# Layer 3's attention: where weights and first rows lie, when queries are masked, and the rhythm of the experts' steps

## The chip, the cores and the metric

The kernel runs on one core of one Trainium2 chip. A core has five engines with queues of their own: PE (TensorE, matrix products), DVE (VectorE), ACT (ScalarE), POOL (GpSimd) and SP (SyncE, which here only issues transfers). They share an on-chip memory (SBUF, 128 partitions) and the accumulators of PE (PSUM, eight banks). The metric is the device time of one execution in microseconds (us); a lower time is better. The version before takes 1958.88 us, the median of 4 runs.

## The reference

Four layers follow each other on 16 sequences (NB) of 256 tokens (T) with 128 features (D). Each layer normalises its input and adds to it an attention and a feed-forward part:

```python
xn = layernorm(x)
x = x + attention(xn) + ffn(xn)
```

The change is in layer 3. Its attention has 16 heads of 8 features. Queries with little energy are set to zero before the scores, and softmax is taken over all 256 keys:

```python
q, k, v = split(xn @ w_qkv.T + b_qkv)               # 16 heads of hd = 8
energy = norm(q, axis=-1)
mask = energy > energy.mean() * 0.1
scores = einsum('bihd,bjhd->bijh', q, k) / sqrt(hd) * mask[:, :, None, :]
probs = softmax(scores, axis=2)                     # over the keys j
attention = einsum('bijh,bjhd->bihd', probs, v) @ w_out.T + b_out
```

Its feed-forward part sends every token to the one of 8 experts (128 to 512 to 128 features, ReLU between) whose gate is largest.

## The kernel before

Tokens are kept as 32 blocks of 128 (X, partition = token in its block). Layer 3 has three stages.

**The front** (L2431 to L2584) normalises X to XN (norm, L2440, even blocks on DVE, odd ones on ACT), transposes four blocks at a time to xnT (turn, L2451), multiplies them by the weights (products, L2456: qT and kT feature-major, V token-major, and the gate logits L), and takes the energies EN (energy, L2480). Eight such groups g of 512 tokens follow each other. Then comes the routing: the threshold thr, the mask of the first queries, counts per expert with products pcnt and pcum, and from them pos, the slot of every token, and ewi, the rows of the experts' weights. A mask(g) (L2415) is one DVE operation that zeroes the queries of one group in qT, and one store of them to DRAM (q_d) on SP. heads_in(g) (L2421) loads queries and keys of the group (two sequences) back from q_d and k_d into QEs and KEs, with 8 features and a row of maxima on each quarter of the partitions. The front ends with 32 scatters on POOL (L2579), which write the rows of XN to their slots (xs_d), one after the other.

**The loop** (L2761 on, U, LAG and LATE are set there) runs u from -6 to 67. Steps 0 to 63 are the four steps s of each sequence b. A step has two halves (par), each with two heads' transposed scores pE (PE), their exponentials PT (ACT), and, six steps ahead (LAG), the same heads' scores pM, of which DVE takes the row maxima mx (L2781). values (L2614) multiplies the exponentials of the step before by V into pc, copies pc to cs every second step and sends it through DRAM (c_d) to Y and den; divide, spread and project finish a sequence. The steps u = -6 to -1 compute pM and mx alone: they are called the lead here. maxima_out (L2639) sends the maxima to the queries' spare row.

**The experts** are a generator. For each of NTL = 23 tiles of 256 slots POOL gathers the tile's weights ex and loads its rows xt, PE multiplies in 5 steps (pt, two ph, pf, po), and POOL scatters the result yo to ya_d. The loop takes one step (next(moe)) in each half once the count of halves exceeds LATE; u = 0 has the halves 13 and 14. After the 115th step rows_in (L2728) loads the results in four parts, waits two further steps and adds a part to X in each of four steps.

What sets the order. Within layer 3 the instructions of DVE, PE and ACT run in the order in which the program emits them (manual_schedule); the order on SP and POOL is chosen by a scheduler. Tiles lie in pools that are laid out one behind the other. The first use of a new pool waits for the last use of every older pool whose room it overlaps, in SBUF as in PSUM. Before the change, l3_big (qT, XN, V, EN, pos, ewi, thr) lies over the room of layer 2's large tiles (l2_big), and l3_w (weights, VEs, QEs, KEs, slot) partly over that of layer 2's temporaries (l2_tmp: statistics, accumulated rows, hidden tiles). The front's PSUM pool l3_ps has two banks each with tags t (transposes, pt) and q (pq, pcnt, pbo), two banks for v and one for e (energies, pcum). The loop's pool l3_ps2 takes all eight banks again, so the first pM waits for the last reader of the front's, the bias add of L2574.

The masks' places, and the steps of the experts, are these lines of the loop:

```python
if 2 <= u + LAG < 8:
    mask(u + LAG)
half += 1
if half > LATE:
    next(moe, None)
```

Of the kernel before, what the change touches and what calls it, by code (L numbers as in the profile page):

```python
# [9 lines left out]
F32 = mybir.dt.float32  # L10
I32 = mybir.dt.int32
AF = mybir.ActivationFunctionType
ALU = mybir.AluOpType
AX = mybir.AxisListType
PSUM = bass.MemoryType.PSUM
DRAM = bass.MemoryType.DRAM

P = 128
NB = 16
T = 256  # L20
D = 128
NT = NB * T // P
# [143 lines left out]
def layer0(tc, I, kit, X):  # L166
# [3 lines left out]
    with ExitStack() as ctx:  # L170
# [51 lines left out]
        stats = {}  # L222
        V, S = nc.vector, nc.scalar

# [6 lines left out]
        def rows_of(th, g):  # L231
            return Xv[:, 4 * g : 4 * g + 4, th, :]

        def norm_stats(th, g, part):
# [6 lines left out]
            for i in (2 * part, 2 * part + 1):  # L241
                V.bn_stats(st[:, i, :], rows_of(th, g)[:, i, :])
                V.bn_aggr(mv[:, i, :], st[:, i, :])
            if part == 1:

                rs = tmp.tile([P, 2, 4], F32, name="rs", bufs=8)
                V.tensor_scalar(rs[:, 1, :], mv[:, :, 1], 1.0 + 1e-6, 1e-11, ALU.mult, ALU.add)
                V.tensor_scalar(rs[:, 0, :], mv[:, :, 1], 1e-5, None, ALU.add)
                rsf = rs.rearrange("q a n -> q (a n)")
# [3 lines left out]
        def norm_rows(th, g):  # L253
# [6 lines left out]
            if th == 0:  # L260
                for i in range(4):
                    V.tensor_scalar(
                        xr[:, i, :], src[:, i, :], mv[:, i, 0:1], rs[:, 1, i : i + 1], ALU.subtract, ALU.mult
# [2102 lines left out]
def layer3(tc, I, kit, X, xs_d, ov):  # L2366
    nc = tc.nc
    H, HD, E, HF = 16, 8, 8, 4
    TS, NTL = L3_TS, L3_NTL
    scale = 1.0 / math.sqrt(HD)  # L2370
    vec, act = nc.vector, nc.scalar
    with ExitStack() as ctx:
        big = ctx.enter_context(tc.tile_pool(name="l3_big", bufs=1))
        wp = ctx.enter_context(tc.tile_pool(name="l3_w", bufs=1))
        tmp = ctx.enter_context(tc.tile_pool(name="l3_tmp", bufs=2))

        qT = big.tile([P, NT * P], F32, name="qT")

        XN = big.tile([P, NT, D + 1], F32, name="XN")
        V = big.tile([P, NT, D], F32, name="V")  # L2380
        EN = big.tile([P, NT * P], F32, name="EN")
        pos = big.tile([P, NT], I32, name="pos")
        ewi = big.tile([P, NTL], I32, name="ewi")
# [14 lines left out]
        boc = wp.tile([P, 1], F32, name="boc")  # L2398
        nc.sync.dma_start(boc, I["L3_attn_b_out"].unsqueeze(1))

        VEs = [wp.tile([P, 2, H, 32], F32, name=f"ve{i}") for i in range(2)]


        QEs = [wp.tile([P, 4, 2 * T], F32, name=f"qe{i}") for i in range(2)]
        KEs = [wp.tile([P, 4, 2 * T], F32, name=f"ke{i}") for i in range(2)]

        slot = wp.tile([P, 2 * NTL], F32, name="slot")
        dram = ctx.enter_context(tc.tile_pool(name="l3_dram", bufs=1, space=DRAM))
        q_d = dram.tile([P, NT * P], F32, name="q_d")
        k_d = dram.tile([P, NT * P], F32, name="k_d")  # L2410
# [4 lines left out]
        def mask(g):  # L2415

            cols = slice(512 * g, 512 * g + 512)
            vec.scalar_tensor_tensor(qT[:, cols], EN[:, cols], thr, qT[:, cols], ALU.is_gt, ALU.mult)
            nc.sync.dma_start(q_d[:, cols], qT[:, cols])
# [13 lines left out]
        with ExitStack() as c1:  # L2433
            en = c1.enter_context(tc.tile_pool(name="l3_en", bufs=1))
            ps = c1.enter_context(tc.tile_pool(name="l3_ps", bufs=2, space=PSUM))
            es = en.tile([P, 8], F32, name="es")
            L = en.tile([P, NT, E], F32, name="L")
            xnT, sq = {}, {}
# [10 lines left out]
                        )  # L2449

            def turn(g):  # L2451
                pn = kit.transpose4(ps, XN[:, 4 * g : 4 * g + 4, 0:D], "t")
                xnT[g] = en.tile([P, 4 * P], F32, name="xnT", bufs=3)
                vec.tensor_copy(xnT[g], pn)

# [23 lines left out]

            def energy(g):  # L2480
                cols = slice(512 * g, 512 * g + 512)
                pe = ps.tile([P, 512], F32, name="pe", tag="e", bufs=1)
                nc.tensor.matmul(pe, kit["group8"], sq[g], start=True, stop=True)
                act.activation(EN[:, cols], pe, AF.Sqrt, scale=float(HD), accum_out=es[:, g : g + 1])

            nc.gpsimd.tensor_scalar(XN[:, :, D], kit["token"], 1.0, None, ALU.add)
            norm(0)
            norm(1)
            turn(0)
            for g in range(8):  # L2490
                if g < 6:
# [23 lines left out]
            et = en.tile([P, 1], F32, name="et")  # L2515
            vec.tensor_tensor(L, L, mx.unsqueeze(2).to_broadcast([P, NT, E]), ALU.is_equal)
            vec.tensor_reduce(et, es, AX.X, ALU.add)
            pt = ps.tile([P, 1], F32, name="pt", tag="t")
            nc.tensor.matmul(pt, kit.ones, et, start=True, stop=True)
            vec.scalar_tensor_tensor(  # L2520
                L, L, -float(E), kit["iota"][:, 0:E].unsqueeze(1).to_broadcast([P, NT, E]), ALU.mult, ALU.add
# [6 lines left out]
            vec.tensor_tensor(OH, L, mx.unsqueeze(2).to_broadcast([P, NT, E]), ALU.is_equal)  # L2528

            OHf = OH.rearrange("p n e -> p (n e)")  # L2530
            pcnt = ps.tile([P, NT, E], F32, name="pcnt", tag="q")
            nc.tensor.matmul(pcnt.rearrange("p n e -> p (n e)"), kit.ones, OHf, start=True, stop=True)
            pcum = ps.tile([P, NT, E], F32, name="pcum", tag="e", bufs=1)
            nc.tensor.matmul(pcum.rearrange("p n e -> p (n e)"), kit["triu"], OHf, start=True, stop=True)
            pbo = ps.tile([P, 1], F32, name="pbo", tag="q")
            nc.tensor.matmul(pbo, wo, bqkv[:, 2:3], start=True, stop=True)
            seg = en.tile([P, E, NT], F32, name="seg")
            nc.gpsimd.memset(seg, 1.0)
# [6 lines left out]
            ni = en.tile([P, E], I32, name="ni")  # L2545
            vec.tensor_scalar(ni, inc[:, :, NT - 1], float(TS - 1), None, ALU.add)
            vec.tensor_scalar(ni, ni, 8, None, ALU.logical_shift_right)
            nt = en.tile([P, E], F32, name="nt")
            vec.tensor_copy(nt, ni)
            end = en.tile([P, E], F32, name="end")  # L2550
# [19 lines left out]
            vec.tensor_reduce(ej, past, AX.X, ALU.add)  # L2570
            vec.tensor_scalar(ej, ej, float(E - 1), float(P), ALU.min, ALU.mult)
            vec.tensor_scalar(ewi, ej, kit["token"][:, 0:1], None, ALU.add)

            vec.tensor_tensor(boc, boc, pbo, ALU.add)  # L2574
            mask(1)
            heads_in(1)
            sent = []
# [8 lines left out]
        with ExitStack() as c2:  # L2586
            exp = c2.enter_context(tc.tile_pool(name="l3_ex", bufs=4))
            at = c2.enter_context(tc.tile_pool(name="l3_at", bufs=2))
            ps = c2.enter_context(tc.tile_pool(name="l3_ps2", bufs=1, space=PSUM))
# [61 lines left out]
            def divide(b):  # L2651
                nc.vector.reciprocal(St.den[b], St.den[b])
# [102 lines left out]
            def work():  # L2755
                yield from experts()
                yield from rows_in()

            moe = work()

            U, LAG, LATE = 4 * NB, 6, 20  # L2761
            half = 0
            for u in range(-LAG, U + 4):
                b, s = divmod(u, 4)
                bm, sm = divmod(u + LAG, 4)
                alone = u < 0 or bm >= NB
                for pars in ((0, 1),) if alone else ((0,), (1,)):

                    Ms, Es = [], []
                    for par in pars:  # L2770
                        tags = "me" if par == pars[0] else "em"
                        if bm < NB:
                            Ms.append((ps.tile([P, 2, 2, T], F32, name="pM", tag=tags[0]), bm, sm, par))
                        if 0 <= u < U:
                            Es.append((ps.tile([P, 2, 2, T], F32, name="pE", tag=tags[1]), b, s, par))
                    scores(Ms, Es)
                    for pM, _, _, par in Ms:
                        if sm == 0 and par == 0:
                            St.mx[bm] = at.tile([P, H, 2], F32, name="mx")
                        h0 = 4 * sm + 2 * par  # L2780
                        vec.tensor_reduce(St.mx[bm][:, h0 : h0 + 2, :], pM, AX.X, ALU.max)  # L2781
                    for pE, _, _, par in Es:
                        if par == 0:
                            St.PT[b, s] = at.tile([P, 4, 2, T], F32, name="PT")
                        r0 = 2 * (1 - par)
                        act.activation(St.PT[b, s][:, r0 : r0 + 2], pE, AF.Exp, scale=scale)  # L2786
                    for par in pars:
                        if par == 0:
                            if 1 <= u <= U:
                                values(*divmod(u - 1, 4))  # L2790
                            if s == 2 and 0 <= b + 1 < NB:
                                act.copy(
                                    VEs[(b + 1) % 2][:, :, :, 0:HD],
                                    V[:, 2 * b + 2 : 2 * b + 4, :].rearrange("p i (h d) -> p i h d", h=H),
                                )
                                maxima_out(b + 1)
                            if s == 0 and b % 2 == 0 and 0 < b // 2 < NB // 2 - 1:
                                heads_in(b // 2 + 1)
                            if 2 <= u + LAG < 8:
                                mask(u + LAG)  # L2800
                        half += 1
                        if half > LATE:
                            next(moe, None)

                        if 0 < b <= NB:
                            if (s, par) == (2, 1):
                                divide(b - 1)
                            if (s, par) == (3, 0):
                                spread(b - 1)
                            if (s, par) == (3, 1):  # L2810
                                project(b - 1)
# [88 lines left out]
```

## Time and profile before

| what | value |
|---|---|
| runs | 1959.68, 1958.08, 1943.73, 1961.63 us; median 1958.88 |
| the profiled execution | own time 1960.44 us, span 1958.5 us, mean granted TensorE clock 0.839 |
| hand-over from layer 2 | last DVE operation of layer 2 at 1459.93, first product pq at 1462.72 us |
| routing on DVE | 1499.3 to 1509.9 us |
| 32 scatters on POOL | 1508.3 to 1548.9 us |
| lead, from its first to the loop's first maxima | 1511.86 to 1571.42 us |
| loop with the experts' steps | to 1928.15 us (last yo) |
| end of the span | 1958.5 us |

The profile is one execution seen by the hardware profiler. A line of its timeline has the start in us, the length, the engine, the source line, the operation, the tile written and the tiles read, the shape, how many instructions are taken together, and in brackets how long the engine was idle before and what ended that. A group's line has the busy time of all its instructions, the mean of one in ns, and the idle time before them with its releasers. "issue" means that nothing in the profile explains the wait, "remote" that the releaser is not known. The span leaves out some 2 us of the execution's own time. A matmul's row gives its dispatch and a modelled end; when it is really done shows only in when those who wait for it go on.

### The profile page before, as it was taken

The numbers are of one execution on the slowest core, as the hardware profiler recorded it, in microseconds if no ns is written. First come the engines' busy times: TensorE is split into PE (matmuls) and PEld (weight loads), VectorE is DVE, ScalarE is ACT, GpSimd is POOL, SyncE is SP. The second block draws the span as 40 slices with busy tenths as digits, with TensorE's granted clock in tenths as the row PEclk, the third lists the DMA queues.
The fourth block names the chain that finished last, engine by engine and source line by source line (L and its number), as shares of the span: only waits on it lengthen the run. The fifth ranks groups of instructions, "written<-read, shape, count | busy, mean of one in ns | idle before, by whom it ended". The sixth has DMA issues, their size and how long they took to land.

```text
span 1958.5 us, 26353 instructions
## 1 busy us (share of the span) xinstructions
PE 1515.1 (77%) x8176; PEld 926.0 (47%) x8176; DVE 1338.5 (68%) x4656; ACT 821.6 (42%) x1908; POOL 635.3 (32%) x901
## 2 busy tenths in 40 slices
PE   6686666676675598999988888687887289999995
PEld 3365455554554453444435454344444145555553
DVE  5688999889888537887855567654366266666663
ACT  3555454555555113223324445343443044454442
POOL 4222312213120323343413030556672613333310
PEclk9667766767676668999998999898988589999998
DMA  3121001000000451101102000022222313333314
GB/s 106 26 83 24 12 14 47 18 11 15 13 16 3 89 106 46 44 22 44 22 0 39 8 1 1 18 43 47 41 57 84 106 58 90 103 100 93 106 54 120
DMA packets 114978, 94.43 MB, mean 48 GB/s; under 512 B 35463, under 2 KB 97799, under 8 KB 114599
## 3 DMA queue, kind: packets, MB, share of 16 engines
q1 hardware_dynamic: 94172, 64.20, 12.8%
q0 software_dynamic: 13056, 26.21, 5.4%
q10 hardware_dynamic: 7610, 2.35, 0.5%
q8 instruction: 65, 1.06, 0.2%
q14 instruction: 75, 0.61, 0.1%
HBM read 55.65 MB, written 37.01 MB: 47 GB/s over the span
## 4 chain that ended last, share of the span: by engine, by line
PE 44%; DVE 11%; POOL 5%; issue 4%; DMA 2%; ACT 1%; another core or an unknown queue 0%; ACTq 0%; SPq 0%; POOLq 0%; DVEq 0%
PE pM L2606 6%; PE pc L2619 3%; PE pf L1433 3%; PE ph L2282 3%; PE pf L2265 2%; PE ph L1425 2%; DVE mx L2781 2%; PE pf L2708 2%; PE pk L1392 2%; PE ph L2701 2%; PE tr L151 2%; POOL tok L2168 1%; PE pk L1391 1%; DVE x L143 1%; PE pE L2606 1%
## 5 line engine op out<-in xcount | busy, mean ns | idle before, releaser
L2781 DVE TENSOR_REDUCE mx<-pM 128x4 f32<-128x1024 f32 x128 | 155.1, 1215 | 129.6 <-PE pE L2606 82.2
L2606 PE MATMUL pM<-ke,qe 31*128 31x256 f32 x1024 | 156.4, 433 | 73.4 <-issue 34.3
L2786 ACT ACTIVATE PT<-pE 128x1024 f32<-128x1024 f32 x128 | 130.3, 1023 | 168.0 <-PE pE L2606 166.2
L2606 PEld LDWEIGHTS pM<-ke,qe 31*128 31x128 f32 x1024 | 95.9, 199 | 115.5 <-DVE mx L2781 55.0
L2606 PE MATMUL pE<-qe,ke 32*128 32x256 f32 x1024 | 147.1, 406 | 0.6 <-issue 0.2
L940 ACT ACTIVATE SA<-e,y 16x1 f32<-16x1 f32 x256 | 74.9, 292 | 132.4 <-DVE e L939 105.3
L976 ACT ACTIVATE iR<-SA,A,CR 16x1 f32<-16x1 f32 x240 | 92.5, 386 | 53.0 <-DVE A L945 37.9
L808 PE MATMUL pP<-KB,M 128*128 128x64 f32 x224 | 61.0, 408 | 49.8 <-ACT M L690 49.8
L1131 POOL TENSOR_SCALAR KA<-KT,aS 128x128 f32<-128x128 f32 x128 | 74.5, 601 | 64.0 <-ACT aS L1103 64.0
L2606 PEld LDWEIGHTS pE<-qe,ke 32*128 32x128 f32 x1024 | 92.2, 187 | 4.5 <-ACT PT L2786 1.8
L740 POOL COPY KB<-K 64x256 f32<-64x256 f32 x30 | 11.8, 395 | 247.5 <-PE pP L808 246.6
L1373 POOL TENSOR_TENSOR kv<-qk,v 128x1024 f32<-128x1024 f32 x32 | 65.8, 2057 | 40.9 <-PE pf L1433 10.9
L808 PEld LDWEIGHTS pP<-KB,M 128*128 128x128 f32 x224 | 50.7, 304 | 59.1 <-ACT M L690 59.0
L1427 ACT ACTIVATE e<-ph,eb 128x512 f32<-128x512 f32 x64 | 44.1, 689 | 76.8 <-PE ph L1425 76.1
L2720 POOL DMA_INDIRECT ya_d<-yo,own x46 | 45.6, 992 | 81.1 <-DVE yo L2718 74.1
L1399 DVE TENSOR_REDUCE y<-pr 128x64 f32<-128x512 f32 x64 | 69.2, 1081 | 2.2
L2619 PE MATMUL pc<-PT,ve 128*32 128x256 f32 x1024 | 70.3, 393 | 0.0
L1392 PE MATMUL pk<-kv,tab 128*128 128x512 f32 x128 | 68.4, 626 | 0.0
L292 PE MATMUL pn<-tab,xn 128*128 128x128 f32 x32 | 14.2, 457 | 69.4 <-POOL xn L284 69.4
L1425 PE MATMUL ph<-xnT,ew 128*128 128x512 f32 x128 | 66.8, 603 | 0.0
L1433 PE MATMUL pf<-e,ew 128*128 128x512 f32 x128 | 64.1, 593 | 0.0
L945 DVE SCALAR_TENSOR_TENSOR A<-CR,e,A 16x33 f32<-16x33 f32 (+3 forms) x240 | 57.5, 240 | 8.5
(603 smaller groups left out, 4210.1 us busy)
## 6 DMA issues: line engine op xcount, KB each, us to landing
WB<-w_d SPq DMA_DIRECT2D x8, 1024.0 KB
c_d<-cs SPq DMA_DIRECT2D x16, 512.0 KB
ew<-in_L_ffn_W SPq DMA_DIRECT2D x16, 256.0 KB
xs_d<-zero SPq DMA_DIRECT2D x1, 2967.0 KB
xt<-xs_d POOLq DMA_DIRECT2D x23, 129.0 KB
xrow_d<-XN SPq DMA_DIRECT2D x4, 548.0 KB
X<-in_x SPq DMA_DIRECT2D x4, 512.0 KB
VA<-v_d SPq DMA_DIRECT2D x64, 32.0 KB
```

The source lines that it names most:

```text
L808: nc.tensor.matmul(Run.pP[p // 4][:, o : o + 64], M[:, p, :], KB[:, p].rearrange("q h k -> q (h k)"), start=p % 4 == 0, stop=False, skip_g ...
L940: nc.scalar.activation(s, e, AF.Sqrt, bias=y, scale=-1.0)
L976: nc.scalar.activation(iR, s, AF.Sqrt, bias=A[:, 17:18], scale=SB[:, t, 17:18])
L1131: nc.gpsimd.tensor_scalar(KA[:, p, :], KT[:, p, :], Run.aS[:, p : p + 1], None, ALU.mult)
L1392: nc.tensor.matmul(pkf, kit["triu"], St.kv[n][:, hs], start=i == 0, stop=True)
L1399: nc.vector.tensor_reduce(St.y[n][:, hh], pr.rearrange("p h e f -> p h f e"), AX.X, ALU.add)
L1425: nc.tensor.matmul(ph, ew1[:, e, k * P : (k + 1) * P], xg, start=True, stop=True)
L1433: nc.tensor.matmul(pf, ew2[:, e, k, :], he[q], start=False, stop=False)
L2606: nc.tensor.matmul(out[:, k, i, :], A[rows, s, c + i * P : c + i * P + P], B[rows, s, c : c + T], start=True, stop=True,)
L2619: nc.tensor.matmul(St.pc[32 * r : 32 * r + 32, s % 2, :], VEs[b % 2][:, k, 4 * s + r, :], St.PT[b, s][:, r, k, :], start=k == 0, stop=k == 1,)
L2781: vec.tensor_reduce(St.mx[bm][:, h0 : h0 + 2, :], pM, AX.X, ALU.max)
L2786: act.activation(St.PT[b, s][:, r0 : r0 + 2], pE, AF.Exp, scale=scale)
```

## The change

Four edits, all in layer3.

1. Rooms. A new pool l3_first with qT and V lies first, then l3_w with the weights alone, then l3_big with the rest, to which VEs, QEs, KEs and slot now belong. The first two lie over l2_big only, and l3_big lies over both l2_big and l2_tmp.
2. Banks. The transposes and pt, pbo get a pool of their own (psT, two banks, 6 and 7), and the energies, pcum and pcnt another (psE, two banks, 4 and 5); q and v lie in banks 0 to 3. The add of the bias boc is moved from behind ewi to before the tiles are counted.
3. Masks. Masks 0 and 1 stay in the front. Masks 2 to 7 move from u = -4 to 1 to u = 4, 12, 20, 28, 36 and 44, each four steps before its heads_in.
4. Experts. LATE is 23 instead of 20, and each 16th half takes a second step.

```diff
+        first = ctx.enter_context(tc.tile_pool(name="l3_first", bufs=1))
+        wp = ctx.enter_context(tc.tile_pool(name="l3_w", bufs=1))
         big = ctx.enter_context(tc.tile_pool(name="l3_big", bufs=1))
-        wp = ctx.enter_context(tc.tile_pool(name="l3_w", bufs=1))
         tmp = ctx.enter_context(tc.tile_pool(name="l3_tmp", bufs=2))
-        qT = big.tile([P, NT * P], F32, name="qT")
+        qT = first.tile([P, NT * P], F32, name="qT")
+        V = first.tile([P, NT, D], F32, name="V")
         XN = big.tile([P, NT, D + 1], F32, name="XN")
-        V = big.tile([P, NT, D], F32, name="V")
...
-        VEs = [wp.tile([P, 2, H, 32], F32, name=f"ve{i}") for i in range(2)]
+        VEs = [big.tile([P, 2, H, 32], F32, name=f"ve{i}") for i in range(2)]
...
-        QEs = [wp.tile([P, 4, 2 * T], F32, name=f"qe{i}") for i in range(2)]
+        QEs = [big.tile([P, 4, 2 * T], F32, name=f"qe{i}") for i in range(2)]
...
             ps = c1.enter_context(tc.tile_pool(name="l3_ps", bufs=2, space=PSUM))
+            psE = c1.enter_context(tc.tile_pool(name="l3_psE", bufs=1, space=PSUM))
+            psT = c1.enter_context(tc.tile_pool(name="l3_psT", bufs=2, space=PSUM))
...
-                pn = kit.transpose4(ps, XN[:, 4 * g : 4 * g + 4, 0:D], "t")
+                pn = kit.transpose4(psT, XN[:, 4 * g : 4 * g + 4, 0:D], "t")
...
-            pcnt = ps.tile([P, NT, E], F32, name="pcnt", tag="q")
+            pcnt = psE.tile([P, NT, E], F32, name="pcnt", tag="x")
...
-            pcum = ps.tile([P, NT, E], F32, name="pcum", tag="e", bufs=1)
+            pcum = psE.tile([P, NT, E], F32, name="pcum", tag="e")
...
-            pbo = ps.tile([P, 1], F32, name="pbo", tag="q")
+            pbo = psT.tile([P, 1], F32, name="pbo", tag="t")
...
             vec.tensor_scalar(ni, ni, 8, None, ALU.logical_shift_right)
+
+            vec.tensor_tensor(boc, boc, pbo, ALU.add)
             nt = en.tile([P, E], F32, name="nt")
...
             vec.tensor_scalar(ewi, ej, kit["token"][:, 0:1], None, ALU.add)
-
-            vec.tensor_tensor(boc, boc, pbo, ALU.add)
             mask(1)
...
-            U, LAG, LATE = 4 * NB, 6, 20
+            U, LAG, LATE = 4 * NB, 6, 23
...
-                            if 2 <= u + LAG < 8:
-                                mask(u + LAG)
+                            if u > 0 and u % 8 == 4 and u // 8 + 2 < 8:
+                                mask(u // 8 + 2)
                         half += 1
                         if half > LATE:
                             next(moe, None)
+                            if half % 16 == 0:
+                                next(moe, None)
```

More of the change, by code (lines that the diff above doesn't have):

```diff
@@ L2399, in layer3 @@
         nc.sync.dma_start(boc, I["L3_attn_b_out"].unsqueeze(1))
-        VEs = [wp.tile([P, 2, H, 32], F32, name=f"ve{i}") for i in range(2)]
-        QEs = [wp.tile([P, 4, 2 * T], F32, name=f"qe{i}") for i in range(2)]
-        KEs = [wp.tile([P, 4, 2 * T], F32, name=f"ke{i}") for i in range(2)]
-        slot = wp.tile([P, 2 * NTL], F32, name="slot")
+        VEs = [big.tile([P, 2, H, 32], F32, name=f"ve{i}") for i in range(2)]
+        QEs = [big.tile([P, 4, 2 * T], F32, name=f"qe{i}") for i in range(2)]
+        KEs = [big.tile([P, 4, 2 * T], F32, name=f"ke{i}") for i in range(2)]
+        slot = big.tile([P, 2 * NTL], F32, name="slot")
         dram = ctx.enter_context(tc.tile_pool(name="l3_dram", bufs=1, space=DRAM))
@@ L2481, in energy @@
                 cols = slice(512 * g, 512 * g + 512)
-                pe = ps.tile([P, 512], F32, name="pe", tag="e", bufs=1)
+                pe = psE.tile([P, 512], F32, name="pe", tag="e")
                 nc.tensor.matmul(pe, kit["group8"], sq[g], start=True, stop=True)
@@ L2517, in layer3 @@
             vec.tensor_reduce(et, es, AX.X, ALU.add)
-            pt = ps.tile([P, 1], F32, name="pt", tag="t")
+            pt = psT.tile([P, 1], F32, name="pt", tag="t")
             nc.tensor.matmul(pt, kit.ones, et, start=True, stop=True)
```

## The prediction

> **What bounds the kernel now.** I read the page first, then the groups of the stretch where layer 3's attention begins (1508 to 1572 us), then that stretch's timeline engine by engine, then the hand-over from layer 2, the loop and the tail. On the page, layer 3's scores and the maxima taken from them are the costliest pair:
>
> ```profile
> PE 1515.1 (77%) x8176; PEld 926.0 (47%) x8176; DVE 1338.5 (68%) x4656; ACT 821.6 (42%) x1908; POOL 635.3 (32%) x901
> ...
> L2781 DVE TENSOR_REDUCE mx<-pM 128x4 f32<-128x1024 f32 x128 | 155.1, 1215 | 129.6 <-PE pE L2606 82.2
> L2606 PE MATMUL pM<-ke,qe 31*128 31x256 f32 x1024 | 156.4, 433 | 73.4 <-issue 34.3
> ```
>
> The shares hide what the change touches. The groups of 1508 to 1572 us (busy, mean ns, idle before and its releasers) show a lead in which neither engine works half the time, while POOL sends 32 scatters:
>
> ```profile
> L2579 POOL DMA_INDIRECT xs_d<-XN,pos x32 | 31.1, 972 | 43.9 <-DVE past L2563 34.4 <-issue 8.8 <-DMA xs_d<-XN,pos 0.6
> L2606 PE MATMUL pM<-ke,qe 31*128 31x256 f32 x104 | 21.8, 677 | 45.2 <-issue 28.9 <-DVE mx L2781 10.8 <-DVE boc L2574 5.5
> L2781 DVE TENSOR_REDUCE mx<-pM 128x4 f32<-128x1024 f32 x13 | 15.4, 1220 | 44.7 <-remote 36.0 <-PE pM L2606 7.2 <-PE pE L2606 1.5
> ```
>
> DVE's timeline of the same stretch (start, length, idle before in brackets):
>
> ```profile
> 1509.12 0.74 DVE L2418 SCALAR_TENSOR_TENSOR qT<-EN,thr,qT 128x512 f32<-128x512 f32 x1
> 1511.86 2.36 DVE L2781 TENSOR_REDUCE mx<-pM 128x4 f32<-128x1024 f32 x2 [2.00 <-PE pM L2606]
> 1516.39 2.35 DVE L2781 TENSOR_REDUCE mx<-pM 128x4 f32<-128x1024 f32 x2 [2.18 <-PE pM L2606]
> 1526.92 1.23 DVE L2781 TENSOR_REDUCE mx<-pM 128x4 f32<-128x1024 f32 x1 [8.18 <-remote]
> 1529.74 1.23 DVE L2781 TENSOR_REDUCE mx<-pM 128x4 f32<-128x1024 f32 x1 [1.59 <-remote]
> 1530.88 0.74 DVE L2418 SCALAR_TENSOR_TENSOR qT<-EN,thr,qT 128x512 f32<-128x512 f32 x1
> 1557.82 2.36 DVE L2781 TENSOR_REDUCE mx<-pM 128x4 f32<-128x1024 f32 x2 [26.19 <-remote]
> 1560.09 0.74 DVE L2418 SCALAR_TENSOR_TENSOR qT<-EN,thr,qT 128x512 f32<-128x512 f32 x1
> 1562.35 2.35 DVE L2781 TENSOR_REDUCE mx<-pM 128x4 f32<-128x1024 f32 x2 [1.52 <-PE pM L2606]
> ```
>
> And PE's:
>
> ```profile
> 1517.67 3.21 PE L2606 MATMUL pM<-ke,qe 31*128 31x256 f32 x16 [1.32 <-issue]
> 1531.02 2.08 PE L2606 MATMUL pM<-ke,qe 31*128 31x256 f32 x14 [1.60 <-issue]
> 1559.10 3.21 PE L2606 MATMUL pM<-ke,qe 31*128 31x256 f32 x16 [25.99 <-issue]
> ```
>
> An undisturbed step of the lead repeats after 4.53 us (1511.86 to 1516.39): two maxima, 2.35, and PE's wait, 2.18. A mask does not lengthen it: 1557.82 to 1562.35 is 4.53 too, with the mask inside, because DVE would idle there anyway (1.52 left of 2.18). The lead is long because PE's matmuls dispatched at 1517.67 and 1531.02 are reported done 6 and 25 us late. The waits are 8.18 + 1.59 + 26.19 = 35.96 us, where 2.18 + 1.52 would be usual, so 32.3 us are lost. The first of them lies before the first mask of the lead (1530.88), and the last ends where POOL's burst of scatters (to 1548.9) and first expert loads (1549.2 to 1557.7) ends. That is an association; the trace does not say what holds PE.
>
> **Part 1, weights and first rows in rooms of their own.** The hand-over reads:
>
> ```profile
> 1459.93 0.18 DVE L135 BATCH_NORM_AGGREGATE mv<-st 128x2 f32<-128x6 f32 x1
> ...
> 1460.31 0.34 SPq L2387 DMA_DIRECT2D wqk<-in_L_attn_w_qkv_T  x1
> ...
> 1462.72 3.75 PE L2460 MATMUL pq<-xnT,wqk 128*128 128x512 f32 x4 [2.30 <-POOL rs L112]
> ```
>
> Now the weights wait for layer 2's temporaries, whose last user is that DVE mv. Afterwards they wait only for layer 2's large tiles, so SP can issue them after its last ac load, about 1452.5, ahead of nothing else of SP's. But XN moves the other way: its room now reaches over the temporaries, so its first rows, which ran from 1449.87 (ACT) and 1454.32 (DVE) in the gaps, wait for the mv at 1460.11. The first product needs both. Latest case: four rows on DVE (4 x 0.33) beside four on ACT (4 x 0.40), 1.6 us, half of the two transposes' 1.97 and a copy of 0.68 put pq at 1463.4, +0.7. Earliest: the whole idle of 2.30 goes. Taking four rows out of DVE's busy queue lets the mv end up to 1.3 earlier, which puts pq at 1462.1; I take -0.4 between -2.3 and +0.7. SP's seven issues (0.34 to 0.49 each) move into its own wait of 7.5 us: nothing. The zeroing of qe, ke, ve on POOL (1.80, 1.80, 0.95, twice) needs the temporaries gone before and after: nothing.
>
> **Part 2, banks and the bias.** With transposes in banks of layer 2's that are free early, the first transpose no longer waits for DVE's X (4.89 us at 1458.45); it waits for XN instead, which is counted above. The separate banks for pt, pcnt, pcum and pbo take nothing off the routing chain, which waits for each product itself (1.3 us for pcnt). The bias add (0.35) moves ahead of the positions: scatters start 0.35 later, and the lead's first matmul needs no longer the bias but L, done at 1506.9. What is late next: the four loads of qe, issued from 1503.14 to 1504.24, land at 1506.2, 1507.4, 1508.4 and 1509.25 in the trace, and each row group needs its own. So the first scores end 1.1 us earlier at most, about 1510.7 for 1511.84, not the 2.3 that the release suggests. If the late completions end with the burst, this goes into the wait: I take 0, ends -1.1 and +0.35 (the burst's later start).
>
> **Part 3, masks.** Six masks of 0.74 leave the lead and the loop's first two steps, where they cost nothing by the row above, and enter the loop at u = 4, 12, ... 44, behind the copy of cs. There DVE idles too:
>
> ```profile
> 1584.86 0.68 DVE L2629 COPY cs<-pc 128x512 f32<-128x512 f32 x1
> 1586.20 1.22 DVE L2781 TENSOR_REDUCE mx<-pM 128x4 f32<-128x1024 f32 x1 [0.66 <-PE pE L2606]
> 1588.67 1.22 DVE L2781 TENSOR_REDUCE mx<-pM 128x4 f32<-128x1024 f32 x1 [1.25 <-PE pE L2606]
> ```
>
> A half with the copy leaves 0.66 us, one with the experts' xT as well 0.32 (at 1596.18), so each mask delays the next maximum by 0.1 to 0.4; xT or yT queued behind it wait 0.74, and PE for them. I take 0.3 x 6 = +1.8, ends 0 and 6 x 0.74 = 4.4. The store on SP (0.32) has some 20 us before its heads_in, four u later: nothing.
> The Trainium skill's page "SBUF — State Buffer" (section "SBUF: two separate sides") speaks against putting them there: a DVE operation with two SBUF inputs and a GpSimd operation that reads SBUF exclude each other, and whoever comes second waits. The trace shows the lock with POOL as loser: emp beside the mask of 1560.09 took 0.74 for 0.21 to 0.23, and all eight masks took 0.739 to 0.751. Were DVE the loser, up to 0.99 (a POOL gather) would be added each time, 5.9 us in all; by the row it is nothing.
>
> **Part 4, the experts' steps.** They begin at half 24 instead of 21 and one extra step falls in halves 32, 48, ... 128, so they end at half 131 instead of 135. Halves without a step repeat after 2.48 us (1586.20 to 1588.67); from 1593.70 to 1902.86 105 halves took 2.94 on average, so a step costs 0.46 at most in a shared half. Three fewer early: -1.4. In the tail a u with two steps took 5.37 (the exponentials at 1916.11, 1921.99, 1926.85), one without 3.24 (1926.85, 1930.09, 1933.32): 1.07 a step, four fewer: -4.3. Seven doubled halves: 0.46 each if hidden as the first is, 1.07 if PE has nothing left to hide it, and 1.07 + 0.66 if PE also misses the alternation (1598.65 to 1601.79 is 3.14 for 2.48). I take 1.07: +7.5, ends 3.2 and 12.1. The adds of the rows come two u earlier too:
>
> ```profile
> 1928.15 0.42 DVE L2718 COPY yo<-po 128x256 f32<-128x256 f32 x1 [1.90 <-PE po L2716]
> ...
> 1937.38 1.22 DVE L2750 TENSOR_TENSOR X<-X,EN 128x1024 f32<-128x1024 f32 x1 [2.88 <-DMA EN<-ya_d]
> ```
>
> The rows come 9.23 us after the last yo; two u of 3.24 pass before the add, so DVE still stops for 2.7 us, now at u = 61 with cs queued behind it: I take +0.8, ends 0 and +2.7. Together +2.6, from -2.5 to +9.1. What follows the last pc, 16 us, is untouched.
>
> **Sum.** -0.4 + 0 + 1.8 + 2.6 = +4.0 on the profiled execution's own 1960.44: 1964.4. That execution lies 1.6 above the runs' median, so against the median the time is 1962.9.
>
> **Rivals.**
> *The late completions vanish.* If what PE waits on is something that moves here (the masks' stores, the lead's banks, qe's and ke's place in memory), 32.3 us and the 1.1 of the earlier start go: 1962.9 - 33.4 = 1929.5. For it: one of the four runs took 1943.73, 15 less, so something of this size comes and goes. Against: the first late completion is before any mask of the lead, and scatters, gathers and scores stay. Half of it would give 1947.
> *A further late completion (slower).* The lead starts a little earlier and the burst a little later, so one more step can fall in the burst, and the last scatters can be held themselves. Another wait of 26.2 gives 1989; above 15.6 us more it decides. Against: the waits ended with the burst, which grows by 0.35 only.
> *The doubled steps are free.* At 0.46 each, the sum is -0.3: 1958.6. The profile has PE at 280.65 of 306 us from 1594 to 1900, which leaves little room for it.
>
> **How the numbers follow.** A measurement of this kernel tells about 1% from no change. The late completions as now: 0.56, with its own range 1950 to 1973 (the terms' ends add up to -5.9 and +14.6, which gives 1953 to 1973, and 3 below for the runs' spread). All gone: 0.24, 1922 to 1938. Half gone: 0.04. A further one: 0.16, 1980 to 1992. The free steps lie inside the first. So faster 0.25 (with a little of the half), same 0.59, slower 0.16. Holding 8 in 10 means taking in the vanished wait and leaving out the further one: 1924 to 1976.
>
> **What would show it.** Right: DVE's waits before the maxima of the third and fourth step of the lead stay above 20 us together and end within 2 us of POOL's first gathers; wqk is issued near 1452.5 while pq starts within 1461 to 1463.5; the first maximum comes near 1510.7; the halves with two steps are about 1 us longer; the last yo is in u = 59. Wrong: a lead of 4.5 us a step (the first rival), a wait at a further step (the second), a mask row above 0.75, or an SP wait before a heads_in of the loop.

## The result, and the profile after

The changed kernel takes 1967.36 us (median of 36 runs, 1955.36 to 1974.63); the kernel before took 1958.08 in the runs beside them (57 runs, 1943.73 to 1970.79). The ratio is 1.0048, with a 95% interval from 1.0038 to 1.0058: slower by half a per cent, 9 us by the medians. The profiled execution took 1967.84, with a span of 1965.5.

From the two profiled executions the difference of 7.0 us in the span divides like this. Each stretch is read from the timelines: the end of layer 2 is the dispatch of its last ph, the first product is pq, the maxima are mx.

| stretch | before | after | difference |
|---|---|---|---|
| start to the last ph of layer 2 | 1448.59 | 1446.93 | -1.7 |
| to the first product | 14.12 | 13.91 | -0.2 |
| to the first maximum of the lead | 49.14 | 48.21 | -0.9 |
| lead, to the first maximum of u = 0 | 59.56 | 57.42 | -2.1 |
| loop, to the last maximum (u = 57) | 337.06 | 346.87 | +9.8 |
| tail, to the end of the span | 50.02 | 52.15 | +2.1 |

The first row is code that the change does not touch. The lead still stands still. These are the groups of the changed kernel from 1505 to 1567 us (busy, mean ns, idle before and releasers), and under them DVE's timeline of the lead:

```profile
L2583 POOL DMA_INDIRECT xs_d<-XN,pos x32 | 30.8, 964 | 43.8 <-DVE past L2569 34.4 <-issue 8.5 <-DMA xs_d<-XN,pos 0.9
L2785 DVE TENSOR_REDUCE mx<-pM 128x4 f32<-128x1024 f32 x13 | 15.5, 1221 | 44.2 <-remote 33.9 <-PE pM L2610 5.7 <-PE pm L2645 2.4
```

```profile
1509.06 2.35 DVE L2785 TENSOR_REDUCE mx<-pM 128x4 f32<-128x1024 f32 x2 [1.12 <-PE pM L2610]
...
1522.14 2.35 DVE L2785 TENSOR_REDUCE mx<-pM 128x4 f32<-128x1024 f32 x2 [5.88 <-remote]
1548.85 1.23 DVE L2785 TENSOR_REDUCE mx<-pM 128x4 f32<-128x1024 f32 x1 [24.36 <-remote]
1553.75 1.23 DVE L2785 TENSOR_REDUCE mx<-pM 128x4 f32<-128x1024 f32 x1 [3.67 <-remote]
1557.41 2.35 DVE L2785 TENSOR_REDUCE mx<-pM 128x4 f32<-128x1024 f32 x2 [2.44 <-PE pm L2645]
```

No mask is left in it, and the waits named remote are 33.9 us instead of 36.0, in the same third and fourth step. What is new stands in the tail. SP's queue and DVE in the changed kernel:

```profile
1928.53 4.08 SPq L2739 DMA_DIRECT2D EN<-ya_d  x4
1932.71 3.03 SPq L2636 DMA_DIRECT2D c_d<-cs  x1
1935.85 2.82 SPq L2756 DMA_DIRECT2D out<-X  x2
1940.85 0.55 SPq L2640 DMA_DIRECT2D Y<-c_d  x1
```

```profile
1923.68 0.42 DVE L2722 COPY yo<-po 128x256 f32<-128x256 f32 x1 [0.25 <-PE po L2720]
...
1927.69 0.69 DVE L2633 COPY cs<-pc 128x512 f32<-128x512 f32 x1 [1.75 <-PE pc L2623]
1932.80 1.23 DVE L2754 TENSOR_TENSOR X<-X,EN 128x1024 f32<-128x1024 f32 x1 [4.42 <-DMA EN<-ya_d]
1934.59 1.22 DVE L2754 TENSOR_TENSOR X<-X,EN 128x1024 f32<-128x1024 f32 x1 [0.57 <-DMA EN<-ya_d]
1940.92 0.69 DVE L2633 COPY cs<-pc 128x512 f32<-128x512 f32 x1 [5.10 <-DMA c_d<-cs]
```

The context of the sequence b = 14 is copied at 1927.69, but its store stands in SP's queue behind the four loads of the experts' rows, 2 MB, which were issued first. It is issued at 1932.71 and landed at 1940.8. The next copy needs the same buffer cs and waits for that: DVE stands still for 5.10 us, and the copies of the last sequence (b = 15) begin that much later. In the kernel before the store was issued at 1923.67, long before the loads (1933.02):

```profile
1923.67 0.37 SPq L2632 DMA_DIRECT2D c_d<-cs  x1
1926.66 0.55 SPq L2636 DMA_DIRECT2D Y<-c_d  x1
1927.27 0.57 SPq L2637 DMA_DIRECT2D den<-c_d  x1
1933.02 4.11 SPq L2735 DMA_DIRECT2D EN<-ya_d  x4
```

### The profile page after: what moved, and what is told of

It reads as the page before. It is cut to its first block, busy times and chain, and to the rows that moved or that the text cites. A ratio compares the mean times of both kernels' runs of the same rounds, so it can differ in the third digit from the quotient of the medians.

```text
span 1965.5 us, 26357 instructions
## 1 busy us (share of the span) xinstructions
PE 1517.3 (77%) x8176; PEld 923.1 (47%) x8176; DVE 1342.3 (68%) x4656; ACT 822.8 (42%) x1908; POOL 635.0 (32%) x901
## 4 chain that ended last, share of the span: by engine, by line
PE 43%; DVE 12%; POOL 4%; issue 3%; DMA 3%; another core or an unknown queue 2%; ACT 1%; SPq 0%; ACTq 0%; POOLq 0%; DVEq 0%
PE pM L2610 6%; PE pc L2623 3%; PE pf L1433 3%; PE ph L1425 2%; DVE mx L2785 2%; PE ph L2282 2%; PE pf L2265 2%; PE pk L1392 2%; PE pf L2712 2%; PE ph L2705 2%; PE tr L151 2%; POOL tok L2168 1%; PE pk L1391 1%; DVE x L143 1%
## 5 line engine op out<-in xcount | busy, mean ns | idle before, releaser
L2724 POOL DMA_INDIRECT ya_d<-yo,own x46 | 45.6, 992 | 77.9 <-DVE yo L2722 60.6
```

## The experiments

My theory after this: the loss is the experts' rhythm in the loop and the order of the transfers in the tail; the late completions in the lead belong to the burst of scatters and not to anything that the change moves. The rival: the masks in the loop cost the 9.8 us, and the lead's waits are the lead's own. The twelve kernels ran in three batches of four, each batch on one chip, beside runs of the kernel before on the same chip. Unless said otherwise a kernel is the changed one with the edit shown. "Lead", "loop" and "tail" are the stretches of the table.

### First batch (kernel before: 1962.19 us)

**Loads two steps later.**

```diff
                 ygs = []
+                for _ in range(2):
+                    yield
                 for g in range(4):
```

> The changed kernel with one edit: the loads of the experts' rows come two steps later, so that SP takes the store of the second to last sequence's context first. If SP's order costs the tail (that store was issued at 1932.7, behind loads issued from 1928.5, with its data ready at 1928.4, and landed at 1940.8), the store lands within 4 us again, the stretch from the loop's last row maximum to the end falls from 52.2 us to 46 to 48, and the time to about 1962. If instead the shared transfers, and not the order, make it late, the stretch stays above 51 and the time at 1967.

1966.59 us, ratio 1.0005 (0.9981 to 1.0029); lead 58.4, loop 345.1, tail 49.7. The edit did not do what it was for: SP's order, chosen by the scheduler, still had three of the four loads ahead of the store (issued at 1932.71, its copy at 1929.56), and the next copy waited 10.52 us for it. Open until the third batch.

**The rhythm of before.**

```diff
-            U, LAG, LATE = 4 * NB, 6, 23
+            U, LAG, LATE = 4 * NB, 6, 20
...
-                            if half % 16 == 0:
-                                next(moe, None)
```

> The changed kernel with the experts' rhythm of before (start at half 21, no second steps); rooms, banks and masks as changed. If the rhythm makes the loss, the loop from its first to its last row maximum falls from 346.9 us to within 2 us of the 337.1 of before, the tail to about 50, and the time to 1956 to 1959. If the masks in the loop make it, the loop stays above 343 and the time above 1963.

1962.46 us, ratio 0.9999 (0.9970 to 1.0028). The loop takes 337.99 us: 0.93 more than before, put down here to the six masks (the fronts differ too), and 8.88 less than in the changed kernel, which is nearly all the rhythm's. These are single profiled executions: the kernel above, whose loop is the changed one's, took 345.1, so 7.1 more than here. The tail is 51.5, 1.4 more than before with the same rhythm, so a difference of that size between two tails says little. The rival on the masks falls. The times of this batch alone would not show it, for the kernel above has the rhythm and stands at 1.0005; the second batch gives 1.0039 with the rhythm and 0.9991 without.

**24 scatters held until the lead is over, and all 32.** In both, a scatter depends on the last maximum of the lead:

```diff
+            def scatter(n, dep):
...
+                tc.add_manual_dep(ins.ins, dep.ins.name, ...)
...
+                    if u == -1:
+                        for n in range(8, NT):      # range(NT) when all are held
+                            scatter(n, red)
...
-            U, LAG, LATE = 4 * NB, 6, 23
+            U, LAG, LATE = 4 * NB, 6, 33
...
-                            if half % 16 == 0:
+                            if half % 8 == 0:
```

> The changed kernel with 8 of the 32 scatters where they were and 24 held by a wait on the lead's last row maximum; the experts start at half 34, with a second step in each eighth half. If PE's late completions belong to the burst of scatters, the lead goes on at 4.5 us a step after the eighth scatter (about 1516), lasts 27 us from its first maximum to the loop's first instead of 57.4, and the waits named remote vanish from it; what they become in the loop is open. If they belong to the lead itself, 20 us or more of them stay and the lead lasts over 45. Time, in the first case, 1930 to 1945 if the loop does not take the wait over, up to 1970 if it does.

> As the kernel with 24 held scatters, but all 32 are held. If the burst makes the late completions, the lead shows none and lasts 25 to 29 us; if the number in flight (eight fit before POOL first waits) decides, this and the other kernel differ by under 2 us in the lead. If scatters stall PE in the loop as much as in the lead, the loop's first 20 steps lengthen by 20 us or more and the time is 1960 to 1975; if PE keeps its pace there, 1930 to 1945.

Times 1973.63 (ratio 1.0051, 1.0014 to 1.0088) and 1984.48 (1.0109, 1.0069 to 1.0149). The profiled execution of the first was its fastest, 1958.13: its last ph of layer 2 came at 1432.56, 14 us earlier than in the changed kernel, and the late completions are in it all the same. The waits follow the burst. DVE's timeline with 8 scatters in the lead and 24 after it:

```profile
1501.43 2.36 DVE L2796 TENSOR_REDUCE mx<-pM 128x4 f32<-128x1024 f32 x2 [2.33 <-PE pM L2621]
1509.97 2.36 DVE L2796 TENSOR_REDUCE mx<-pM 128x4 f32<-128x1024 f32 x2 [6.18 <-remote]
1514.51 2.36 DVE L2796 TENSOR_REDUCE mx<-pM 128x4 f32<-128x1024 f32 x2 [2.18 <-PE pM L2621]
...
1536.16 1.22 DVE L2796 TENSOR_REDUCE mx<-pM 128x4 f32<-128x1024 f32 x1 [3.41 <-PE pE L2621]
1560.26 1.23 DVE L2796 TENSOR_REDUCE mx<-pM 128x4 f32<-128x1024 f32 x1 [22.88 <-remote]
```

And with all 32 after it:

```profile
1532.82 2.36 DVE L2792 TENSOR_REDUCE mx<-pM 128x4 f32<-128x1024 f32 x2 [2.18 <-PE pM L2617]
...
1580.71 1.23 DVE L2792 TENSOR_REDUCE mx<-pM 128x4 f32<-128x1024 f32 x1 [34.07 <-remote]
```

After the first 8 scatters (and the four gathers of weights that then move up) PE's completion is 4.0 us late, in the burst of 24 it is 20.4 late, in that of 32 30.7, each counted from the modelled end of PE's last matmul to the start of the maximum that needs it. With no scatter in it the lead takes 27.2 us at 4.53 a step, and the loop pays instead. The rival on the lead falls in this batch: the waits come with the burst of POOL's transfers, in the lead or in the loop, and moving it only moves them.

### Second batch (kernel before: 1929.44 us)

**Scatters spaced out.** A scatter for each maximum, or two for each in the loop. The experts begin after the last scatter: from half 37 with 16 second steps, or from half 27 with 7:

```diff
+                        if len(sent) < NT:
+                            scatter(len(sent), red)
```

> The changed kernel with each scatter held by a wait on one row maximum, one for each half from the lead on (a scatter each 2.3 us in the lead, each 2.5 to 3.4 us in the loop), the experts from half 37 with a second step in each sixth half. The runs with held scatters showed the late completions in the burst wherever it lies, 4.0 us after 8 scatters, 20.4 us in a burst of 24 and 30.7 us in one of 32. If back-to-back scatters make them, pacing removes them: the lead lasts 27 us from its first maximum to the loop's first, and the 16 second steps cost about 16 us, so the time is 1943 to 1955. If each scatter costs PE about 1 us whatever its spacing, the lead lasts 35 to 40 us, the loop's first ten steps 15 to 20 us more than usual, and the time is 1970 or above.

> As the kernel paced one by one, but two scatters for each half of the loop (each 1.4 us), done at half 22, with the experts from half 27 and a second step in each sixteenth half. If only unbroken bursts hold PE, the lead is the same 27 us, the loop's first five steps lose little and the time is 1935 to 1948. If pairs hold PE too, the first five steps lengthen by 10 to 20 us and the time is 1955 to 1970.

**Loads four steps later**, the edit above with 4 for 2:

> The changed kernel with the loads of the experts' rows four steps later, so that they are issued in the half in which the kernel before issued them. With two steps the store of the context still stood behind three of the four loads and landed at 1940.7. If the collision of loads and store makes the tail's loss, the store is issued within 1 us of its copy and the stretch from the loop's last row maximum to the end falls from 52.2 us to 45 to 47, the time to about 1961. If it stays above 50, something else holds the tail.

**Rooms, banks and bias alone:**

```diff
-                            if u > 0 and u % 8 == 4 and u // 8 + 2 < 8:
-                                mask(u // 8 + 2)
+                            if 2 <= u + LAG < 8:
+                                mask(u + LAG)
```

with the rhythm of before as well.

> The kernel before with the rooms, the banks and the earlier bias add alone; masks and the experts' rhythm as before. By the prediction nothing that can be measured: first product 0 to 1 us earlier beside layer 2, scatters and the lead's end with them, loop and tail as before, time within 3 us of the kernel before. If the masks in the lead lengthened PE's late completions, its lead is some us longer than the changed kernel's 57.4 (to 59.6 as before); if not, the difference of the two leads is as large as that between two executions.

| kernel | time | ratio (interval) | lead | loop | tail |
|---|---|---|---|---|---|
| one scatter a half | 1949.21 | 1.0109 (1.0037 to 1.0180) | 27.2 | 355.3 | 50.9 |
| two a half in the loop | 1935.63 | 1.0033 (1.0008 to 1.0058) | 27.2 | 340.5 | 49.2 |
| loads four steps later | 1938.11 | 1.0039 (1.0008 to 1.0070) | 27.2 | 341.5 | 50.3 |
| rooms, banks, bias alone | 1928.36 | 0.9991 (0.9955 to 1.0026) | 27.2 | 333.9 | 48.7 |

This batch ran on another chip, and it upset the half of the theory that had seemed settled: here the lead is 27.2 us in every kernel, also in the two whose 32 scatters follow each other without a gap beside it. No profiled execution shows a completion that is more than half a us late, and the kernel before, with its burst in the lead, is 33 us faster than in the first batch. So in these runs no late completion came without the burst, but the burst came without them. The pacing can't be judged here, since there was nothing to gain: it shows only what its rhythm costs, 6.6 us in the loop with 7 second steps and 21.4 with 16, each against the kernel with rooms, banks and bias alone.

What the batch does show: rooms, banks and the bias move nothing that can be measured, as forecast (the interval is 0.7% wide); the rhythm costs 7.6 us of the loop with the masks in it (341.5 against 333.9); and moving the loads four steps later still leaves the store behind three of them (the next copy waited 10.65 us).

### Third batch (kernel before: 1920.13 us)

**SP's order fixed.** The loads two steps later, and behind the store by an edge that orders SP's queue without a wait:

```diff
-                    nc.sync.dma_start(c_d[b].rearrange("s r c t -> (r c) s t"), St.cs[b])
+                    St.cd = nc.sync.dma_start(c_d[b].rearrange("s r c t -> (r c) s t"), St.cs[b])
...
+                    tc.add_manual_dep(load.ins, St.cd.ins.name, ...NoSync...)
```

> The changed kernel with the loads of the experts' rows two steps later and, in SP's order, behind the store of the second to last sequence's context; two earlier kernels moved the loads two and four steps and left that order as it was (store issued behind three loads, landed 10 us after its copy). If order makes the tail's loss, the store lands 3 to 4 us after the copy, the stretch from the loop's last row maximum to the end falls from 52.2 and 49.8 us to 44 to 47. If the sequence's context is held by the shared transfers in any order, it stays above 49. Against the kernel before on its own chip: a ratio of 1.000 to 1.003 in the first case, 1.004 or more in the second.

1924.09 us, ratio 1.0022 (1.0004 to 1.0039); tail 46.6, loop 341.5. SP's queue and the copies on DVE:

```profile
1891.16 0.37 SPq L2636 DMA_DIRECT2D c_d<-cs  x1
1891.82 1.49 SPq L2741 DMA_DIRECT2D EN<-ya_d  x2
1894.70 0.55 SPq L2640 DMA_DIRECT2D Y<-c_d  x1
```

```profile
1890.44 0.69 DVE L2633 COPY cs<-pc 128x512 f32<-128x512 f32 x1 [1.69 <-PE pc L2623]
1896.91 0.69 DVE L2633 COPY cs<-pc 128x512 f32<-128x512 f32 x1 [5.78 <-PE pc L2623]
```

The copies follow each other after 6.5 us instead of 13.2, the second waits for PE again, and the store has landed 3.5 us after its issue instead of 8.1, with two of the loads right behind it. So it was the order that held the copy, not the sharing. The tail is 5.6 us shorter than the changed kernel's, but the order alone does not give all of that: the two edits that moved the loads in time without moving them in the queue changed the tail by 2.4 and 1.9 us, and against the first of them, which differs by the edge alone, the tail is 3.2 shorter (49.7 and 46.6, one execution each, from different batches). The times do not show the 3.2: the two ratios, 1.0005 and 1.0022, agree within their intervals. The kernel is still no faster than the one before: the loop's second steps remain.

**Two scatters a half, masks in the lead:** the paced kernel above with the masks of before.

> Rooms and banks as changed, masks in the lead as before, one scatter held by each row maximum of the lead and two by each of the loop, experts from half 27 with a second step in each sixteenth half. On the chip where neither kernel showed late completions, the same pacing cost 0.3%, all of it the experts' rhythm. If this chip shows late completions in the burst (see the lead of the kernel with the tail's order, sent with it) and spacing avoids them, the lead is 27 us and the ratio 0.985 to 0.992; if each scatter costs PE its microsecond anyway, the lead or the loop's first five steps are 20 us longer and the ratio is 1.003 to 1.01.

1929.32 us, ratio 1.0036 (1.0019 to 1.0053); lead 27.2, loop 340.2. Against the paced kernel with masks in the loop, which differs in the masks alone, they are 0.4 us of its 340.5.

**Plain transfers to fixed places, by POOL and by SP.** They start when the slots are known, as the scatters do, but leave the sorting out: the experts work on other tokens than the gate chose.

```diff
-                ins = nc.gpsimd.indirect_dma_start(
-                    xs_d, bass.IndirectOffsetOnAxis(ap=pos[:, n : n + 1], axis=0), XN[:, n, :], None
+                ins = nc.gpsimd.dma_start(xs_d[n * P : n * P + P], XN[:, n, :])    # or nc.sync
```

> The changed kernel with the 32 scatters replaced by 32 plain transfers of the same rows from POOL's queue, to fixed places instead of the slots (the experts then work on other tokens than the gate chose; the amount of work is the same). If POOL's making of descriptors holds PE, and this chip shows late completions, they stay with the plain transfers from POOL and the lead lasts over 45 us. If the gathering of offsets in the indirect form does it, they vanish and the lead is 27 us, or less than 20 us of burst.

> The same plain transfers to fixed places, issued by SP instead of POOL. If the transfers' traffic itself holds PE, the late completions stay (lead over 45 us). If it is POOL's part in them, the lead is 27 us and, on a chip that shows late completions, the kernel is 1.2 to 1.8% below the one before; on a chip without them 0.3 to 0.6% above.

1930.82 us (ratio 1.0053, 1.0029 to 1.0076) and 1935.31 (1.0074, 1.0047 to 1.0100); leads 28.4 and 32.2. Neither can answer its question: again no kernel of the batch shows a late completion, the one with the tail's order and its full burst included (lead 27.2). This third batch ran on the same chip as the first. So the chip alone does not decide. DVE's timeline of the lead in the kernel with the order fixed, its 32 scatters beside it from 1504.88 to 1545.24:

```profile
1507.48 2.36 DVE L2793 TENSOR_REDUCE mx<-pM 128x4 f32<-128x1024 f32 x2 [1.12 <-PE pM L2610]
1512.02 2.36 DVE L2793 TENSOR_REDUCE mx<-pM 128x4 f32<-128x1024 f32 x2 [2.18 <-PE pM L2610]
1516.55 2.35 DVE L2793 TENSOR_REDUCE mx<-pM 128x4 f32<-128x1024 f32 x2 [2.18 <-PE pM L2610]
1521.08 2.36 DVE L2793 TENSOR_REDUCE mx<-pM 128x4 f32<-128x1024 f32 x2 [2.18 <-PE pM L2610]
...
1534.68 1.22 DVE L2793 TENSOR_REDUCE mx<-pM 128x4 f32<-128x1024 f32 x1 [2.18 <-PE pE L2610]
```

The traces differ in one more thing, and it goes with the waits in all fourteen. In the profiles of the kernel before, of the changed one and of the first batch, the page's list of transfers gives no time from issue to landing for POOL's loads xt; in the eight of the two later batches it gives 2.7 to 3.2 us. The first line is the kernel before, the second the one with the order fixed:

```profile
xt<-xs_d POOLq DMA_DIRECT2D x23, 129.0 KB
xt<-xs_d POOLq DMA_DIRECT2D x23, 129.0 KB, 2.7
```

The time is missing because updates of the eight semaphores on which POOL's 196 transfers land are missing: the profile of the kernel before has 2057 of them, that of rooms, banks and bias alone 3096. Whether this belongs to what holds PE, follows from it, or comes with it from the way an execution was recorded, no run tells.

The 5 us that SP's version adds to the lead have another cause: the maxima's store stands behind 28 transfers in SP's queue, and the first pE waits 4.94 us for it.

No version measured beats the kernel before.

## Why the prediction was right, point by point

The forecast was 1962.9, no change within 1% the likeliest, and the likeliest case came: 1967.36, slower by 0.5%, with the late completions as before. Against the profiled execution's 1960.44 the sum was +4.0; the profile shows +7.4. The total hides the terms that failed: the tail above all, and the early steps of the experts.

- **Hand-over, -0.4.** Measured -0.2 from the last ph to the first product. The weights were issued at 1451.14, nine us earlier than before, and it helped nothing, because the first rows of XN (1458.37 on ACT, 1458.42 on DVE) waited for layer 2's last mv, as said. The kernel with rooms and banks alone agrees (ratio 0.9991), but its interval can't resolve a term of this size.
- **Banks and bias, 0.** The first maximum came 0.9 us earlier after the first product (forecast: 1.1 at most, by the landings of qe). The scatters did not start 0.35 later, as its other end had it: they began 45.6 us after the first product in both kernels. Whether the burst took the 0.9 back can't be told: the lead itself was 2.1 shorter, but two kernels of the first batch with the same front have 58.4 and 59.6, so this is the spread of the late completions.
- **Late completions unchanged, 0.56.** Right, and their tie to the burst, called an association, was shown for the first batch by moving the burst. What the prediction did not see is that they can be absent from a whole batch. The reason that it gave for the rival, one run of 1943.73, need not be a sign of that: the kernel with 24 held scatters had an execution 15.5 us below its median with the late completions in it, and what it had gained lay before layer 3's attention.
- **Masks, +1.8.** Measured +0.9 between two kernels that differ in the front as well, and 0.4 between the two paced ones that differ in the masks alone: mis-sized, but within its ends. All eight masks took 0.740 to 0.752 us, in the loop too. With the loads four steps later, two masks of the loop (1567.98 and 1807.42) met a small operation of POOL's: the masks took 0.743 and 0.745, POOL's operations 0.61 and 0.59 instead of 0.20. So POOL and not DVE lost, as the prediction read from its row.
- **The experts' rhythm in the loop, +6.1 (-1.4 and +7.5).** Measured +8.9 against the kernel with the old rhythm; 1.0 of it arose at u = 1, before either has a step (a half of 3.77 us for 2.76), so 7.9 belong to the rhythm. In the second batch it is 7.6 with the masks' 0.4, so 7.2. The size was off in the first part, the -1.4. The three early halves gave nothing back: from the first maximum of u = 0 to that of half 31 the changed kernel took 52.4 us and the one with the old rhythm 51.1, so without that 1.0 still 0.3 more, with three steps fewer; in the second batch the stretch took 51.5 us with either rhythm. What a step costs on average over the shared halves, 0.46, was not what leaving out three early ones saves. The second steps then cost 7.6, 1.1 each, near the 1.07 taken. In half 32, pf is followed by po, which needs yT from DVE: PE stood idle for 0.64 us, and the half took 4.08 instead of 2.5.
- **The tail, -3.5 (-4.3 and +0.8).** Measured +2.1 against before, and this is the step that failed most. The prediction priced the adds' wait on DVE ("DVE still stops for 2.7 us, now at u = 61 with cs queued behind it") and did not ask what the loads, moved two u earlier on SP, are queued in front of. The store of the context was behind them, and the next copy waited 5.10 us for it. With the loads two steps later and behind the store the tail is 5.6 us shorter, of which the order has about 3.2. It is then 3.4 below the kernel before's and 2.1 below that of rooms, banks and bias alone, which comes near the forecast; tails of the old rhythm lie between 48.7 and 51.5.

Together the experts' part was +2.6, from -2.5 to +9.1, and came to 11.0, outside its own range. The stretches before the loop gave back 4.9 in these two executions, where the prediction had 0.4; 3.8 of that lie in layer 2, which nothing changed, and in the lead with its late completions. So it is partly luck that the sum came as near as it did, and the overall range held because it had to take in the late completions.

## What to carry to other kernels

When a step that issues transfers is moved, list what each queue held at the old place and holds at the new one; here loads that waited for nothing critical went ahead of a store whose buffer the next step needed, and moving them in the program by two or four steps did not bring them behind the store, an explicit edge did. The average cost of a step does not price leaving one out or doubling one: here three fewer early steps saved nothing, and a second step in a half cost 1.1 us; in the half looked at, its two parts depend on each other through DVE. Before building on a long stall, see whether it is there in another batch, on the same chip too.

## What the runs showed of the hardware

- PE's completions were late beside a burst of transfers issued by POOL, by 4.0, 20.4 and 30.7 us for bursts of 8, 24 and 32 scatters with the loads that follow, in the lead or in the loop alike; in two later batches, one of them on the chip of the first, the same burst cost PE nothing. With spaced scatters it was not tried in a batch that had the stall. The late matmuls were not waiting for their instructions: in the kernel before they are dispatched by 1532.5, and from 1519 to 1576 us no packet of an instruction queue is listed. The batches with the stall also have the longer loops, 346.9 and 337.1 us where the same loops took 341.5 and 333.9 in the later ones, and profiles with fewer updates of POOL's semaphores. What holds PE, and what differs between batches, stays open.
- Normalising two blocks on DVE took 2.08 and 4.39 us beside POOL's memsets (at 1460.71 and 1466.71), 0.6 without them:

```profile
1460.71 2.08 DVE L2447 TENSOR_SCALAR XN<-X,mv,rs 128x128 f32<-128x128 f32 x2
...
1466.71 4.39 DVE L2447 TENSOR_SCALAR XN<-X,mv,rs 128x128 f32<-128x128 f32 x2
...
1472.91 0.59 DVE L2447 TENSOR_SCALAR XN<-X,mv,rs 128x128 f32<-128x128 f32 x2
```

  The Trainium skill's page "SBUF — State Buffer" (section "SBUF: two separate sides") has DVE and GpSimd share a port pair as an exclusive lock, held for a whole instruction; rows of 2 and 4 us beside memsets of 1.80 agree with that, and here DVE was the loser.
